# Reordering at a megakernel's joints: an add, a table-loading exponential, routing numbers and the first expert's transposes

## The chip, the cores and the metric

The kernel is one program on 1 core of a Trainium2 chip. Its metric is device time in microseconds (us). A profiled execution gives, beside it, the span of the core's recorded work and the share of full clock that TensorE was granted.

Engines are named as in the profile: PE is TensorE, PEld its weight loads, DVE is VectorE, ACT is ScalarE, POOL is GpSimd, and SP is the engine whose queue issues most loads and stores. Each works through its own queue of instructions in order and waits on semaphores for the others.

## The reference, cut to what matters

Two layers act on x (8, 256, 512), that is T = 2048 rows of 512 numbers, with a context of the same shape.

```python
# layer 0
x = x + (relu(n @ wg) * group_norm(A @ V)) @ wo       # n = layernorm(x); 4 heads of 128, decay-masked A
n = layernorm(x)
h = silu(bitlinear(n, w1)) * bitlinear(n, w3)         # 512 -> 1408
x = x + bitlinear(h, w2)                              # rows rounded to 8 bits, weights to -1, 0, 1
# layer 1
x = x + mlstm(layernorm(x), ctx, ctx)                 # 16 heads of 32, decays are exponentials of gate sums
r = rmsnorm(x) * norm_w
scores = softmax(r @ gate_w); topk_w, topk_ids = top_k(scores, 4)
# 32 experts of width 256; an expert keeps at most 2*N/E of its rows
out = x + routed(r, topk_ids, topk_w) + (silu(r @ sg) * (r @ su)) @ sd
```

## The kernel before, in words

Rows go in 16 tiles of 128 (`NT`), or in 4 chunks of 512 (`NCH`); `D` is 512, `KD` its 4 blocks of 128, `E` 32 experts, `TOPK` 4. `g.X[i]` holds the residual rows of tile `i` in on-chip memory from end to end. The stages follow one another on PE, and each hands over to the next at a joint.

**Layer 0 attention** (`layer0_attention`). For each tile: gate product `pw`, attended heads `po`, normed heads `y`, their product `wy`, its transposes, the output product `pz` (`output`, L431), and `settled` (L437), which adds `pz` to the residual (L438) and takes the row statistics (`norm_stats`, L127). All of it stands inside `tc.manual_schedule`: there the order of the code is the order of the queues of PE, ACT, DVE, POOL and SP. The stage's end is L497 to L510: output of tile 15, statistics of tile 14, tile 1 normed and rounded for the feed-forward (`ffn_normed`, `ffn_rounded` L545, `quantize` L513), the context rows' mean (`centered`), reciprocal roots of the statistics, and `settled(15)` last of all.

`quantize` is five instructions in a chain: the largest magnitude (DVE), two 128x1 operations for the scale `qs` (DVE), a shift by a large constant (ACT), and the subtraction that leaves the rounded row `xq` (DVE). `ffn_turned` then issues a transposing DMA for `xqT`.

**Feed-forward, joined to layer 1** (`layers_joined`). Each tile has three chunks of products `p` (L1203) for two weights in two banks each; the banks (tag `pqk`) alternate between two, so that a third chunk needs the first one's banks back, which come free when `gated` (L1216) has multiplied the Silu of one by the other. The hidden row is rounded (`largest` L1220, `hidden_rounded`) and, two tiles later, multiplied by the second weight (`py`, L1250). During the last tiles the first steps of layer 1 are woven in. After the loop come `hidden_scale(15)` and `shifted` for the last hidden row, and then the rounds of layer 1.

**Layer 1 attention** (`layer1_rounds`). There are 32 blocks. A block makes decays (`pd` on PE, then the exponential `xe` on ACT, L821), weights `ct` (`pqk` on PE, L844 on DVE), heads and a normed rest. A round has places 0 to 4; two dictionaries in `layers_joined`, `places` and `spread`, say what is done besides at a place (round, place): the last tiles' outputs and adds, and turns: `early` and `behind` (L1463) each transpose a normed query tile (`ft`, L1330), copy it, and start a further normed row (`xn`, L1322).

**Choices** (`choices`, from L1501). It finds each row's four experts, their weights, the counts `pc`, the experts' order by count (`order`, then `rank` by a 32x32 comparison and its sum), the places `pp` and from these the numbers of list and slot. It is a generator, and at each `yield` `all` runs `filler()`: a piece of the shared expert of chunks 0 and 1 (products L1060, gated rows `act` L1069, down product `po` L1080). A piece has matmuls and a rest, and the rest waits in `then` until the next piece's matmuls stand.

**Route** (`route`, from L1590). It makes index rows on POOL (`iota`), casts them on DVE, and builds the lists of rows by expert and slot: 8 `to_list` and 64 `to_slot` one-hot matrices (DVE), whose products `pl` (L1654) give `tok_of`, the rows that each expert gathers, and `to`, where its results go. `is_rank`, `at` and `expert` give the experts' numbers, which SP reads to load their weights. Here no order is written out: a planner places the instructions of `route` and of the shared expert's chunks 2 and 3 (`glu` L1744 to L1749, `down` L1761, `add`, store).

**Experts** (`layer1_ffn`, from L1715). `fetch` (L1786) gathers an expert's rows by an indirect DMA from POOL; `turn` (L1792) takes their weights for this expert (`of`, L1796, with a sum), transposes them (`pt`, L1801) and multiplies by the norm's weights (`xT`, L1802). From `tc.manual_schedule` at L1831 on, PE, ACT and DVE follow the code: the first expert's four turns, then 32 experts, each with two products, Silu, `act`, a down product, scaling `eo` and an indirect add into the output (L1805). Ahead of `route`, POOL clears the output's spare rows with a memset and four DMAs.

Of the kernel before, what the change touches and what calls it, by code (L numbers as in the profile page):

```python
# [30 lines left out]
P = 128  # L31
# [212 lines left out]
def layer0_attention(g, tc, cp, qpool):  # L244
# [7 lines left out]
    with ExitStack() as ctx:  # L252
# [178 lines left out]
        def output(i, of=range(KD)):  # L431
            if 0 in of:
                pz[i] = ps.tile([P, D], F32, tag=f"s{2 + i % 2}", name="pz")
            for k in of:
                nc.tensor.matmul(pz[i], lhsT=wyT[i][:, k, :], rhs=wo[:, k, :], start=k == 0, stop=k == KD - 1)  # L435

        def settled(i):  # L437
            nc.vector.tensor_add(g.X[i], pz.pop(i), g.X[i])  # L438
            norm_stats(g, g.mv[:, i, :], g.X[i])

        def raw_load(i):
# [17 lines left out]
        with tc.manual_schedule(engines={E_.PE, E_.Activation, E_.DVE, E_.Pool, E_.SP}):  # L459
            ternary.load_next()  # L460
            ternary.load_next()
            pw[0] = gate(0)
            for h in range(H0 + 1):
                if h < H0:
                    nc.vector.tensor_mul(AT[h], sums[h], AT[h])
                    nc.scalar.activation(AT[h], AT[h], AF.Abs)
                if h:
                    nc.vector.tensor_scalar(AT[h - 1], AT[h - 1], 1.0, None, ALU.max)
            for i in range(NT - 1):
                paired = i in (0, NT - 2)  # L470
                if i != 1:
                    attended(i)
                    ternary.scale_next(i)
                    normed_heads(i)
                ternary.side(i)
                if i:
                    centered(i - 1)
                raw_load(i)
                pw[i + 1] = gate(i + 1)
                if paired:  # L480
                    attended(i + 1)
                if 1 <= i < NT - 3:
                    values((i + 3) // 2, (i + 1) % 2)
                if i:
                    output(i - 1)
                gated(i)
                if paired:
                    normed_heads(i + 1)
                turned(i)
                if i:  # L490
                    settled(i - 1)
                if i == NT - 2:
                    xn = ffn_normed(g, work, 0)
                ternary.clip()
            late = NT - 1
            gated(late)
            output(late - 1, range(KD - 1))  # L497
            turned(late)
            output(late - 1, range(KD - 1, KD))
            g.begun.append(ffn_turned(g, *ffn_rounded(g, work, xn)))  # L500
            ternary.side(late)
            centered(late - 1)
            raw_load(late)
            output(late)
            settled(late - 1)
            ternary.clip()
            g.begun.append(ffn_turned(g, *ffn_rounded(g, work, ffn_normed(g, work, 1))))
            centered(late)
            roots_of_inputs(g, slice(4, NT - 1))
            settled(NT - 1)  # L510


def quantize(g, out, tmp, x):  # L513


    nc = g.nc
    am = g.small.tile([P, 1], F32, tag="am", name="am")
    nc.vector.tensor_reduce(am, x, AX.X, ALU.max, apply_absolute_value=True)
    inv = g.small.tile([P, 1], F32, tag="qi", name="qi")
    nc.vector.tensor_scalar(inv, am, 1e-5, 1.0 / 127.0, ALU.max, ALU.mult)  # L520
    sc = g.small.tile([P, 1], F32, tag="qs", name="qs")
    nc.vector.reciprocal(sc, inv)
    nc.scalar.activation(tmp, x, AF.Identity, bias=g.eps["magic"], scale=sc)
    nc.vector.tensor_scalar(out, tmp, MAGIC, 127.0, ALU.subtract, ALU.min)
    return inv

# [15 lines left out]
    return xn  # L542


def ffn_rounded(g, work, xn):  # L545

    nc = g.nc
    xq = work.tile([P, D], BF16, tag="xq", name="xq")
    ix = quantize(g, xq, xn, xn)
    s13 = g.fin.tile([P, 2], F32, tag="s13", name="s13", bufs=4)  # L550
    nc.vector.tensor_scalar(s13, g.iw[:, :2], ix, None, ALU.mult)
    return xq, s13
# [200 lines left out]
def layer1_rounds(g, tc, gates, work, ps, qp):  # L753
# [390 lines left out]
    class Rounds:  # L1144
# [20 lines left out]
        def all(self, between):  # L1165
            full = len(blocks) + 3
            for n in range(full + 10):
                if n - full in (-2, -1, 0, 1, 2, 4, 6, 7):
                    filler()
                round_(n, between)  # L1170
            lgT = logits()
            filler()
            logits_turned(lgT)
            for _ in choices(g, work, ps):
                filler()
            while pieces or then:
                filler()

# [3 lines left out]
def layers_joined(g, tc, qp, gates):  # L1182
# [5 lines left out]
    with tc.tile_pool(name="f0a1", bufs=2, reuse_waits="tile") as work, tc.tile_pool(name="f0a1ps", bufs=1, space=PSUM, reuse_waits="tile") as ps:  # L1188
# [20 lines left out]
        def silu(t, n):  # L1209
            p1, _, sg = p[n]  # L1210
            return nc.scalar.activation(sg, p1, AF.Silu, scale=xq[t][1])  # L1211
# [135 lines left out]
        with tc.manual_schedule(engines={E_.PE, E_.Activation, E_.DVE, E_.Pool, E_.SP}):  # L1347
# [15 lines left out]
            for t in range(NT):  # L1363
# [52 lines left out]
                gate_steps(t, 2)  # L1416
                products(t, 2)
                behind = silu(t, 2)
                for ins in {8: gates.picked, 11: partial(later_constants, g)}.get(t, tuple)():
                    tc.add_manual_dep(  # L1420
                        ins.ins, behind.ins.name,
                        mybir.DependencyInfo(mybir.DependencyClass.Sync, mybir.DependencyReason.DATA),
                        reason="in this tile's time",
                    )
# [33 lines left out]
            def turned(tag, engine=None):  # L1458
# [7 lines left out]
                (0, 2): [partial(times, 1, first)],  # L1466
                (0, 1): [partial(rooted, late - 2, 5), partial(hidden_rounded, late), partial(rooted, late - 2), partial(added, late - 1)],
                (0, 4): [partial(times, 1, first), norm_next, norm_next],
                (1, 1): [early],
                (1, 3): [behind],  # L1470
                (1, 4): [partial(stats, late - 1), partial(times, 1, first)],
                (2, 0): [partial(output, late, "back", 1)],
                (2, 1): [partial(added, late), early],
# [27 lines left out]
def choices(g, work, ps):  # L1501
# [50 lines left out]
    for i in range(NT):  # L1552
        nc.tensor.matmul(pc, lhsT=onesb, rhs=mask[:, i, :], start=i == 0, stop=i == NT - 1)
    nc.vector.tensor_copy(count, pc)
    nc.vector.scalar_tensor_tensor(order, col, -1.0 / P, count, ALU.mult, ALU.add)
    nc.vector.tensor_tensor(
        sq, order.unsqueeze(1).to_broadcast(square), order.unsqueeze(2).to_broadcast(square), ALU.is_gt
    )
# [28 lines left out]
    yield  # L1587


def route(g, keep, pool, ps):  # L1590


    nc = g.nc
# [10 lines left out]

    lists_i = new("lists_i", [P, E, NJ], I32)
    nc.gpsimd.iota(lists_i, pattern=[[16, E], [1, NJ]], base=0, channel_multiplier=0)
    slots_of = new("slots_of", [P, E])
    for r in range(E):
        if r == 0 or SLOTS[r] != SLOTS[r - 1]:
            nc.gpsimd.memset(slots_of[:, r:], float(SLOTS[r]))  # L1610
    col = new("col", [P, E])
    nc.vector.tensor_copy(col, iota[:, :E])

    slots = new("slots", [P, P], F16)
    nc.vector.tensor_copy(slots, iota)
    lists = new("lists", [P, E * NJ], F16)
    nc.vector.tensor_copy(lists, lists_i.rearrange("p e j -> p (e j)"))
    row = new("row", [P, 1])
    nc.vector.tensor_copy(row, iop)
    number = new("number", [P, NT])  # L1620
    nc.vector.tensor_scalar(number, col[:, :NT], float(P), 1.0, ALU.mult, ALU.add)
    nc.vector.tensor_scalar(number, number, row, None, ALU.add)
    spare = new("spare", [P, NJ])
    nc.vector.tensor_scalar(spare, col[:, :NJ], float(P), float(T + 1), ALU.mult, ALU.add)
    nc.vector.tensor_scalar(spare, spare, row, None, ALU.add)


    g.is_rank = new("is_rank", square, pool=keep)
    nc.vector.tensor_tensor(
        g.is_rank, rank.unsqueeze(1).to_broadcast(square), col.unsqueeze(2).to_broadcast(square), ALU.is_equal  # L1630
    )
    sq = new("sq", square)
    nc.vector.tensor_mul(sq, g.is_rank, col.unsqueeze(1).to_broadcast(square))
    at = new("at", [P, E])
    nc.vector.tensor_reduce(at, sq, AX.X, ALU.add)
    g.expert = new("expert", [P, E], I32, keep)
    nc.vector.tensor_copy(g.expert, at)


    pl = ps.tile([P, E, NJ], F32, tag="rt", name="pl", bufs=1)  # L1640
    half = NT // 2
    for n in range(2 * TOPK):
# [6 lines left out]
        for i in range(i0, i0 + half):  # L1649
# [5 lines left out]
                pl.rearrange("p e j -> p (e j)"), lhsT=to_slot, rhs=to_list[:, i - i0, :],  # L1655
                start=n == 0 and i == 0, stop=n == 2 * TOPK - 1 and i == NT - 1,
            )


    plf = new("plf", [P, E, NJ])  # L1660
# [54 lines left out]
def layer1_ffn(g, tc):  # L1715
    nc = g.nc
    with ExitStack() as ctx:
# [47 lines left out]
            return [po[h * at : h * at + n, :cols] for h in range(parts)]  # L1765

        zero = work.tile([P, D], F32, tag="eo", name="zero", bufs=3)
        nc.gpsimd.memset(zero, 0.0)
        for j in range(NJ):
            nc.gpsimd.dma_start(out=g.out[T + j * P : T + (j + 1) * P, :], in_=zero)  # L1770
        sg_w, su_w, sd_w = g.shared
        ps = ctx.enter_context(tc.tile_pool(name="f1ps", bufs=2, space=PSUM, reuse_waits="tile"))
        with tc.tile_pool(name="f1rwork", bufs=1, reuse_waits="tile") as rwork:
            route(g, rp, rwork, ps)
        for c in range(EARLY, NCH):
            act = glu(ps, sg_w, su_w, g.qT[c])
            for j in range(CH // P):
                i = c * (CH // P) + j
                (po,) = down(ps, act, sd_w, j)
                nc.vector.tensor_add(g.X[i], po, g.X[i])  # L1780
                nc.sync.dma_start(out=g.out[i * P : (i + 1) * P, :], in_=g.X[i])

        def fetch(r, j, n=P):

            xg = work.tile([P, D + E], F32, tag="xg", name="xg", bufs=6)
# [31 lines left out]
        def turn_block(r, j):  # L1817
# [8 lines left out]
            if r + 2 < E and j < len(BLOCKS[r + 2]):  # L1826
                xg[r + 2].append(fetch(r + 2, j, BLOCKS[r + 2][j]))

        before = []
        E_ = mybir.EngineType  # L1830
        with tc.manual_schedule(engines={E_.PE, E_.Activation, E_.DVE}):  # L1831
            for j in range(NJ):
                turn_block(0, j)
            for r in range(E):
                w13, w2 = load_expert(r)
                act = glu(ps, w13[:, :, :FI], w13[:, :, FI:], xT.pop(r), SLOTS[r], partial(turn_block, r + 1))
# [140 lines left out]
```

## Time and profile before

| | before |
|---|---|
| median of 3 runs | 1031.09 us (1029.36 to 1031.83) |
| profiled execution | 1030.34 us |
| its span | 1028.6 us, 14755 instructions |
| mean granted PE clock | 0.994 |
| busy PE, PEld | 990.8 us (96%), 603.4 us |
| busy DVE, ACT, POOL | 527.2, 404.1, 404.5 us |
| HBM read, written | 110.42 MB, 33.23 MB |

By stage, from the same execution (busy us in each stretch):

| stretch, us | what runs | PE | DVE | ACT |
|---|---|---|---|---|
| 200 to 300 | end of layer 0 attention, feed-forward | 94.85 | 89.41 | 68.00 |
| 300 to 400 | feed-forward's end, layer 1 attention's start | 91.04 | 72.80 | 66.87 |
| 400 to 500 | layer 1 attention | 97.18 | 84.07 | 73.08 |
| 500 to 600 | shared expert, choices, lists | 95.55 | 80.39 | 18.46 |
| 600 to 800 | experts | 200.00 | 38.65 | 40.05 |
| 800 to 1000 | experts | 200.00 | 39.59 | 47.37 |
| 1000 to 1028.6 | last expert, end | 17.15 | 2.73 | 3.78 |

How to read it: times are microseconds from the span's start. A row of the timeline or of the chain gives start, duration, engine, line and tile; "x8" is the number of instructions in it, and square brackets hold the idle time before it and what ended that. Matmuls are pipelined, so a busy PE is not PE at its peak, and two rows of matmuls may overlap by a little.

### The profile page before, as it was taken

The numbers are of one execution on the slowest core, as the hardware profiler recorded it, in microseconds if no ns is written. First come the engines' busy times: TensorE is split into PE (matmuls) and PEld (weight loads), VectorE is DVE, ScalarE is ACT, GpSimd is POOL, SyncE is SP. The second block draws the span as 40 slices with busy tenths as digits, with TensorE's granted clock in tenths as the row PEclk, the third lists the DMA queues.
The fourth block names the chain that finished last, engine by engine and source line by source line (L and its number), as shares of the span: only waits on it lengthen the run. The fifth ranks groups of instructions, "written<-read, shape, count | busy, mean of one in ns | idle before, by whom it ended". The sixth has DMA issues, their size and how long they took to land.

```text
span 1028.6 us, 14755 instructions
## 1 busy us (share of the span) xinstructions
PE 990.8 (96%) x5220; PEld 603.4 (59%) x5220; DVE 527.2 (51%) x1338; ACT 404.1 (39%) x693; POOL 404.5 (39%) x501
## 2 busy tenths in 40 slices
PE   8999999989999899999999999999999999999995
PEld 6766656534444356666544445555666666778783
DVE  7446566679987858878969831211212221122110
ACT  4443343457776757877430002122122222221221
POOL 0023443430111113788303225455455555444432
PEclk9999999999999999999999999999999999999998
DMA  9853333324332511231116248687788788889983
GB/s 344 294 185 117 141 118 130 103 67 76 60 58 40 92 39 45 64 126 55 62 62 225 82 147 189 169 209 190 182 207 207 207 210 231 220 242 240 230 225 46
DMA packets 101154, 152.67 MB, mean 148 GB/s; under 512 B 39592, under 2 KB 42280, under 8 KB 101036
## 3 DMA queue, kind: packets, MB, share of 16 engines
q1 hardware_dynamic: 82128, 107.04, 34.1%
q0 software_dynamic: 18944, 44.60, 19.4%
q8 instruction: 43, 0.70, 0.3%
q14 instruction: 39, 0.32, 0.1%
HBM read 110.42 MB, written 33.23 MB: 140 GB/s over the span
## 4 chain that ended last, share of the span: by engine, by line
PE 72%; DVE 13%; DMA 4%; POOL 4%; ACT 3%; issue 2%; SPq 0%; POOLq 0%; ACTq 0%; DVEq 0%
PE po L1761 14%; PE pg L1744 13%; PE pu L1744 13%; PE pw L399 5%; PE pz L435 5%; PE pt L1801 3%; PE p L1203 2%; DMA wst<-in_w1T 2%; DVE am L1220 2%; PE pgu L1060 2%; DVE h L1216 2%; DVE ct L844 2%; PE po L415 1%; PE po L412 1%; DVE st L127 1%
## 5 line engine op out<-in xcount | busy, mean ns | idle before, releaser
L1749 DVE TENSOR_TENSOR act<-pu,sg 128x264 f32<-128x264 f32 (+22 forms) x68 | 31.9, 469 | 313.5 <-PE pu L1744 303.2
L1786 POOL DMA_INDIRECT xg<-h_d,tok_of x85 | 83.6, 983 | 196.0 <-DVE of L1796 64.1
L1805 POOL DMA_INDIRECT out_x<-eo,to x85 | 132.9, 1564 | 55.1 <-ACT eo L1843 34.3
L1761 PE MATMUL po<-w,act 128*128 128x512 f32 (+10 forms) x456 | 143.1, 489 | 0.0
L1744 PE MATMUL pg<-xT,w 128*128 128x216 f32 (+21 forms) x512 | 134.9, 406 | 0.7 <-DVE xT L1802 0.7
L1843 ACT ACTIVATE eo<-po,slotw 128x512 f32<-128x512 f32 (+10 forms) x114 | 65.1, 576 | 173.9 <-PE po L1761 166.9
L1744 PE MATMUL pu<-xT,w 128*128 128x216 f32 (+21 forms) x512 | 133.3, 403 | 0.0
L1744 PEld LDWEIGHTS pg<-xT,w 128*128 128x128 f32 x512 | 93.2, 190 | 33.2 <-issue 16.9
L1748 ACT ACTIVATE sg<-pg 128x264 f32<-128x264 f32 (+22 forms) x68 | 28.5, 420 | 213.5 <-PE pg L1744 213.5
L1744 PEld LDWEIGHTS pu<-xT,w 128*128 128x128 f32 x512 | 96.8, 190 | 26.2 <-issue 5.6
L1203 PE MATMUL p<-wq,xqT 128*128 128x512 bf16 (+1 forms) x384 | 82.9, 367 | 6.4 <-DVE qi L1224 3.1
L1761 PEld LDWEIGHTS po<-w,act 128*128 128x128 f32 (+10 forms) x456 | 54.1, 155 | 57.5 <-issue 47.6
L420 POOL TENSOR_TENSOR y<-y,gam 128x512 f32<-128x512 f32 x16 | 20.2, 1265 | 135.5 <-DVE y L81 135.5
L1203 PEld LDWEIGHTS <-xqT 128*128 128x128 bf16 x384 | 37.6, 99 | 50.2 <-issue 13.6
L1802 DVE TENSOR_TENSOR xT<-pt,nw 128x512 f32<-128x512 f32 (+12 forms) x85 | 51.1, 601 | 20.5 <-PE pt L1801 20.5
L435 PE MATMUL pz<-wo,wyT 128*128 128x512 f32 x128 | 57.8, 594 | 0.7 <-ACT wyT L429 0.7
L399 PE MATMUL pw<-wg,xnT 128*128 128x512 f32 x128 | 57.8, 594 | 0.0
L1801 PEld LDWEIGHTS pt<-ident,xg 128*128 128x128 f32 (+15 forms) x340 | 39.1, 140 | 23.6 <-PE po L1761 10.5
L127 DVE BATCH_NORM_STATS2 st<-x 128x6 f32<-128x512 f32 x64 | 43.8, 687 | 9.2 <-POOL x L913 4.5
L1801 PE MATMUL pt<-ident,xg 128*128 128x128 f32 (+15 forms) x340 | 47.0, 260 | 0.6 <-DVE xT L1802 0.5
L844 DVE SCALAR_TENSOR_TENSOR ct<-pqk,xe 128x768 f32<-128x768 f32 x44 | 40.0, 951 | 8.8 <-PE pqk L840 8.1
L1211 ACT ACTIVATE sg<-p,s 128x512 f32<-128x512 f32 (+1 forms) x48 | 31.1, 648 | 28.2 <-PE p L1203 28.1
(338 smaller groups left out, 1678.7 us busy)
## 6 DMA issues: line engine op xcount, KB each, us to landing
w<-in_w SPq DMA_DIRECT2D x32, 1024.0 KB
w<-in_w SPq DMA_DIRECT2D x32, 512.0 KB
wst<-in_w1T SPq DMA_DIRECT2D x8, 704.0 KB
wst<-in_w3T SPq DMA_DIRECT2D x8, 704.0 KB
wst<-in_w2T SPq DMA_DIRECT2D x6, 768.0 KB
x<-in_x SPq DMA_DIRECT2D x16, 256.0 KB
ctxT<-in_ctxT_d SPq DMA_DIRECT2D x4, 1024.0 KB
raw<-in_ctx SPq DMA_DIRECT2D x16, 256.0 KB
```

The costliest lines, as they stand in the source:

```text
L127: first = g.nc.vector.bn_stats(st, x)
L399: nc.tensor.matmul(pw, lhsT=xnT[c][:, k, o : o + P], rhs=wg[:, k, :], start=k == 0, stop=k == KD - 1)
L435: nc.tensor.matmul(pz[i], lhsT=wyT[i][:, k, :], rhs=wo[:, k, :], start=k == 0, stop=k == KD - 1)
L844: nc.vector.scalar_tensor_tensor(ct[:, r : r + 2, :], pqk[:, :, : S + P], 1.0 / math.sqrt(HD1), xe[:, r : r + 2, :], ALU.mult, ALU.mult,)
L1203: nc.tensor.matmul(both[:, m, : z - a], lhsT=xqT[:, k, :], rhs=w[:, k, a:z], start=k == 0, stop=k == KD - 1)
L1744: nc.tensor.matmul(pp[:, :n], lhsT=w[:, k, cols], rhs=xT[:, k, :n], start=k == 0, stop=k == KD - 1)
L1761: nc.tensor.matmul(po[h * at : h * at + n, :cols], lhsT=act[:, m, j * P : j * P + n], rhs=w[:, m, h * cols : (h + 1) * cols], start=m == 0 ...
L1786: nc.gpsimd.indirect_dma_start(out=xg[:n], out_offset=None, in_=h_d, in_offset=bass.IndirectOffsetOnAxis(ap=g.tok_of[:n, r, j : j + 1], ax ...
L1801: nc.tensor.transpose(pt[:, k, :n], xg[:n, k * P : (k + 1) * P], g.ident[:n, :n])
L1802: nc.vector.tensor_mul(xT, pt[:, :, :n], g.nw.unsqueeze(2).to_broadcast([P, KD, n]))
L1805: return nc.gpsimd.indirect_dma_start(out=g.out, out_offset=bass.IndirectOffsetOnAxis(ap=rows, axis=0), in_=eo, in_offset=None, compute_op ...
L1843: nc.scalar.activation(eo[:n, at : at + cols], po, AF.Copy, scale=w[r][:n, j : j + 1])
```

## The change

It has six parts. No instruction's shape changes, and nothing is left out of the computation.

1. `settled` is split. The add of `pz` becomes `summed`, and that of tile 15 is handed through `ffn_rounded` to `quantize`, which runs it between tile 1's shift on ACT and its rounding on DVE. The statistics of tile 15 stay at the end.
2. After the last tile's last Silu, ACT takes an exponential of a constant (128x1).
3. The first turn, `early` at place 1 of round 1, goes to place 3, ahead of `behind`.
4. `choices` yields once more, right after `order`; at that yield only the waiting rest of a piece is run, and no new matmuls.
5. `route` clears the spare rows behind the index rows on POOL, casts `lists` and `slots` first, and makes `spare`, `is_rank`, `at` and `expert` inside the first pass of the list loop.
6. The gathers of the first two experts and the first expert's four turns stand ahead of the down product of tile 14, instead of behind all shared rows.

The diff, cut to its core:

```diff
+        def summed(i):
+            nc.vector.tensor_add(g.X[i], pz.pop(i), g.X[i])
         def settled(i):
-            nc.vector.tensor_add(g.X[i], pz.pop(i), g.X[i])
+            if i in pz:
+                summed(i)
             norm_stats(g, g.mv[:, i, :], g.X[i])
...
-            g.begun.append(ffn_turned(g, *ffn_rounded(g, work, ffn_normed(g, work, 1))))
+            g.begun.append(ffn_turned(g, *ffn_rounded(g, work, ffn_normed(g, work, 1), partial(summed, late))))
...
     nc.scalar.activation(tmp, x, AF.Identity, bias=g.eps["magic"], scale=sc)
+    if between:
+        between()
     nc.vector.tensor_scalar(out, tmp, MAGIC, 127.0, ALU.subtract, ALU.min)
...
-            for _ in choices(g, work, ps):
-                filler()
+            for only_rest in choices(g, work, ps):
+                if not only_rest:
+                    filler()
+                elif then[0]:
+                    then[0]()
+                    then[0] = None
...
                 behind = silu(t, 2)
+                if t == NT - 1:
+                    nc.scalar.activation(g.small.tile([P, 1], F32, tag="sd", name="warm"), g.eps["ln"], AF.Exp)
...
-                (1, 1): [early],
-                (1, 3): [behind],
+                (1, 3): [early, behind],
...
     nc.vector.scalar_tensor_tensor(order, col, -1.0 / P, count, ALU.mult, ALU.add)
+    yield True
...
     nc.gpsimd.iota(lists_i, pattern=[[16, E], [1, NJ]], base=0, channel_multiplier=0)
+    zeros()
...
-    g.is_rank = new("is_rank", square, pool=keep)
...
-    nc.vector.tensor_copy(g.expert, at)
...
+        if n == 0:
...
+            g.is_rank = new("is_rank", square, pool=keep)
...
+            nc.vector.tensor_copy(g.expert, at)
...
+                if i == NT - 2:
+                    for first in range(NJ):
+                        turn_block(0, first)
                 (po,) = down(ps, act, sd_w, j)
...
         with tc.manual_schedule(engines={E_.PE, E_.Activation, E_.DVE}):
-            for j in range(NJ):
-                turn_block(0, j)
             for r in range(E):
```

## The prediction

> **What bounds the kernel now.** I read the page first (busy shares, chain), then the busy time and granted clock of each stage, then the timeline of the four places that the diff touches.
>
> ```profile
> PE 72%; DVE 13%; DMA 4%; POOL 4%; ACT 3%; issue 2%; SPq 0%; POOLq 0%; ACTq 0%; DVEq 0%
> ```
>
> The chain that ends last is mostly TensorE (PE). The stretches from 600 to 1000 us are 100% busy on PE: the experts only shift with whatever comes before them. So I look for idle PE at the joints. First joint, feed-forward's start (timeline of PE, then windows: length, PE busy, granted clock, DMA share, GB/s):
>
> ```profile
> 215.44 1.90 PE L1203 MATMUL p<-wq,xqT 128*128 128x512 bf16 x8
> 219.86 0.38 PE L1203 MATMUL p<-wq,xqT 128*128 128x512 bf16 x1 [2.52 <-DVE x L438]
> ```
> ```profile
> 216.80:220.22 3.42, 0.90 (x5) 1.00 0.70 148
> 220.22:223.63 3.41, 3.41 (x11) 0.50 0.50 107
> 356.75:360.16 3.41, 1.74 (x16) 1.00 1.10 115
> 360.16:363.58 3.42, 3.42 (x22) 0.50 0.01 3
> ```
>
> PE stood 2.52 us until the add of the last output product freed its bank, and after that window, with 0.90 of 3.42 us busy, the clock was 0.50 for 3.41 us: the next eight matmuls ran 0.43 us apart, not 0.215. The same pair of windows comes at 357 to 363 us. Second joint, the attention's start (the first line from ACT's timeline, the others from the chain of waits):
>
> ```profile
> 350.42 1.28 ACT L821 ACT_TABLE_LOAD   x1 [1.30 <-PE pd L817]
> ```
> ```profile
> 357.75 0.80 ACT xn L1322
> 358.55 0.49 ACT xe L821
> 359.08 0.38 PE pd L816
> ...
> 360.80 1.04 PE ft L1330 x4
> ```
>
> The exponential's table is loaded only after the first decays' matmul. The third `pd` waits for an exponential that stands behind two normed rows on ACT. Third joint, choices and lists:
>
> ```profile
> 560.00:580.00 20.00, 20.00 (x83) 9.28 (x83) 20.00 (x59) 1.20 (x2) 0.00 (x0) 1.00 0.21 78
> 541.11 6.28 PE L1080 MATMUL po<-sw,act 128*128 128x512 f32 x14 [1.39 <-DVE act L1069]
> 554.60 0.68 PE L1654 MATMUL pl<-to_list,to_slot 128*128 128x128 f16 x3 [1.21 <-DVE to_slot L1651]
> ```
>
> In the window line the third busy figure is VectorE (DVE): 20.00 of 20.00. It runs from 537.0 to 584.4 us with no gap over 0.1 us. Fourth joint, the first expert:
>
> ```profile
> 588.75 0.19 DVE L1796 SCALAR_TENSOR_TENSOR of<-xg,is_rank 128x32 f32<-128x32 f32 x1 [3.13 <-DMA xg<-h_d,tok_of]
> 588.86 0.08 DVE L1796 DVE_READ_ACCUMULATOR of<-xg,is_rank 128x1 f32 x1
> 589.09 0.69 DVE L1749 TENSOR_TENSOR act<-pu,sg 128x512 f32<-128x512 f32 x1
> ```
>
> One slot weight (`of`, which waits for its gathered rows) already stands ahead of the last shared `act` on DVE.
>
> **Part 1, the last output product's add.** It moves from 219.13 to behind `qs` of tile 1 (ends 216.27); its product ended at 215.43 (10 matmuls from 210.84, 4.59). It then ends at 216.9, before PE's first eight matmuls do (217.34), so the second chunk starts at 217.4 and ends at 219.1 (8 x 0.215). What is late next: the third chunk takes the first one's banks, so it needs the gated rows `h` of the first. Silu ends at 219.38 (ACT, unchanged), but on DVE `h` stands behind `xq`, the mean, and the statistics of tile 15. The add, 0.6 us, now pushes `xq` from 217.22 to about 217.5, and the rest by about 0.2; after the mean (0.67) and small ones the statistics start at 219.3 where they started at 219.84, and `h` runs 220.15 to 220.9 where it ran 220.67 to 221.39. Third chunk: 220.95, where it was 223.3 (219.86 + 8 x 0.43). That is **-2.35 us**; PE stands 1.8 us instead of 2.52. The second tile's transposing DMA is issued 0.3 later, at 218.1; the first tile's took 2.57 from issue (212.87) to matmul (215.44), so it lands at 220.7 and is wanted at 222.25: hidden by the third chunk (1.3 us), without which it would cost nothing until 0.2. DVE's later rows (`xq` of tile 2 at 224.57, the largest of `h` at 226.10) shift alike, so the loop keeps it. Without the half clock in a run of before, its third chunk would start at 221.6 and the gain be 0.65. Both ends, -0.65 and -2.35, go into the range; I take the traced one.
>
> A page bears here: the Trainium skill, "TensorE: Matmul & The Clock Gate", table "Why this matters for your kernels", says that PE idle of more than about 3 us brings the half clock. The trace has it after 2.52 us, so the row decides. By the page alone the half clock would not come from this gap, and the gain would be an estimated 0.65.
>
> **Part 2, the early exponential.** It pulls the 1.28 us load to 349.13, behind the last Silu. ACT idles there (1.30), and the first decays come 1.0 us sooner, at 350.7. I cost it at nothing: from 349.80 to 357.00 the chain is DVE alone (largest of `h`, add, statistics, reciprocal roots in Newton steps, `nb`), and no step of it waits for ACT; the rounded hidden row at 354.83 follows a root step begun at 354.71 (0.17) while ACT's shift ended at 354.24. The cover is that DVE chain; without it, the part is worth -1.0. Below nothing it can't go by more than the small exponential, 0.3 (like the 128x1 root of 0.30 at 207.56).
>
> **Part 3, the first turn.** Four transposes (`ft`, 1.04 for this set, at half clock; 0.45 at full clock, as the next set has it in the chain at 365.79) leave a hole at 357.89, where PE waited anyway: the third `pd` stays at 359.08, since its exponential still follows both normed rows on ACT. They now stand behind the scores, ahead of the last product `py`. So PE's chain to `py` grows by 0.45 to 1.04; with the clock halved for one window in both, I get +0.3 (the idle before it grows to 3.4 us, 355.7 to 359.08, so a half clock is as good as certain). `copy` of that turn on DVE moves behind two `ct` (1.82), into 2.23 us that DVE stood before the add at 365.83: nothing. Normed rows 10 on ACT wait for the moved transposes (two buffers), and the second copy ends about when `py` starts: 0 to 0.1. **+0.3** (0 to +1.0).
>
> **Part 4, gated rows.** `act` (0.69) goes ahead of the comparison and its sum (1.23, 1.22). PE's 1.39 vanishes; DVE's sum to the lists is the same. PE is not what ends here: 0.
>
> **Part 5, lists' numbers.** DVE runs the same operations before `tok_of` in either order (64 `to_slot`, 8 `to_list`, 3 `act`, 7 adds), so `tok_of` still ends near 583.98: 0. The first `to_slot` comes about 2.3 sooner (552.2), but PE reaches it at 549.0 (14 x 0.43 from 539.6, 8 x 0.43), since only four rows of `pg` now stand ahead: 3.2 us idle in place of 1.39 + 1.21, with 2.6 us more work behind it, in a stretch where PE has some 2 us of slack against DVE. A half clock there (1.7 us of lost work) would be mostly covered: 0 to +0.5. POOL: the four zero DMAs (1 MB, 2.18 us of issue) go 0.95 us later, behind the index rows; POOL is idle 32.1 us after that. SP: the experts' numbers come 3.4 us later (556.6), so 3 MB of weights are issued at 557.4 and land near 569 rather than 565.3; wanted at 599.4. That cover is 30 us.
>
> **Part 6, the first expert's turns before the last two tiles.** Removed: after the last product PE spent 3.3 us (596.13 to 599.44) on 16 transposes (1.8) and waits for `xT` (0.51 + 0.05 + 0.74 + small). Now three rows of product (2.6) cover the four `xT` (0.6, 0.6, 0.6, 0.42). Added wait: on DVE three `of` stand ahead of the last `act`. Fetches are issued at 584.27, 585.69, 586.97; the first two took 4.5 and 4.8 to land (588.75, 590.5), the range of all is 2.8 to 4.8, so the third lands at 590.7 to 591.8 (below: 589.8). I take 591.1. `act` ends at 591.8 instead of 589.78; behind it on DVE stand the adds and `xT`, and PE waits for it after one row. From 588.98: 0.86 + 2.0 wait + 7 x 0.86 + 1.8 = 599.7, against 599.44. **+0.4** (-1.3 if nothing waits; +1.0 with the latest landing; half clock +1.7 more).
>
> **Sum.** -2.35 + 0 + 0.3 + 0 + 0.1 + 0.4 = -1.5 us on an execution of 1030.34 (span 1028.6 and 1.74 around it): 1028.8. The median of the three runs, 1031.09, lies 0.75 higher; I forecast half way, **1029.2**.
>
> **Rivals.**
> - Fetches in time: if the second and third gathers land by 589, `act` does not wait and part 6 is -1.5, part 3 nothing: -2.35 - 1.5 = -3.9, 1026.5 to 1027.2. For it: gathers of 2.8 us exist, and fewer writes run beside them. Against: 4.5 and 4.8 are those of this place.
> - The wait takes the gain back: three `of` hold `act` to 592.5 and the clock halves after it. Place: DVE's queue at 589. It decides from a landing of the third fetch past 591.5, PE then stands over 2.5 us as at 217. Price: 1.0 + 1.7; with the small form of part 1 (-0.65), part 3 at 1.0 and part 5 at 0.5: +3.5, 1034.6. For it: the 3.13 us wait is there now. Against: PE had 0.86 us of its own work.
> - The change does nothing as a whole: part 1 is worth only 0.65, and parts 3 and 6 give it back: 0, about 1031.
>
> **How the numbers follow.** Forecast 0.40, in-time fetches 0.30, wait 0.18, nothing 0.12. A difference below 0.3% (3.1 us) can't be told from none here: faster means under 1028.0, slower over 1034.2. Of the forecast's own spread (part 2 or 3 better by 1.0) I count 0.09 as faster: faster 0.39, same 0.31 + 0.12 = 0.43, slower 0.18. The range leaves out about one in ten at each end: 1026.5 to 1033.5; the forecast's own is 1027.5 to 1031.
>
> **What would show it.** Right: no wait of PE on DVE's `x` add near 217, no half clock near 220, third chunk near 221; an ACT table load right behind the last Silu; the last shared `act` near 591 with a PE gap of 2 us ahead of it; experts' first `pg` 1.5 us sooner. Wrong: PE's chain from 220 to 350 not shifted by 2 us; `tok_of` moved by over 1 us against the choices' first row; `act` at 589.

## The result, and the profile after

The changed kernel takes 1032.59 us (median of 20 runs, 1029.84 to 1035.19); the kernel before, in 20 runs, 1029.64 us (1027.52 to 1032.0). The ratio is 1.0027, 95% interval [1.0018, 1.0035]. The medians lie 2.95 us apart: the kernel became slower, where 1.9 us faster than the three runs then shown (median 1031.09) was forecast. The profiled execution took 1033.24 us, span 1031.5 us, granted clock 0.991. Its span is 2.9 us over the one of before, as the medians are, so the two profiles are a fair pair.

The chain of waits at its end, from the page of the changed kernel, has less PE and more VectorE, DMA and issue:

```profile
PE 70%; DVE 14%; DMA 5%; POOL 4%; ACT 3%; issue 3%; SPq 1%; POOLq 0%; DVEq 0%; ACTq 0%
```

Windows of the changed kernel (length, PE busy, granted clock, DMA share, GB/s), in pairs: a joint, and what follows it.

```profile
216.80:220.22 3.42, 2.63 (x13) 1.00 0.65 151
220.22:223.63 3.41, 1.89 (x10) 1.00 0.78 128
353.88:357.29 3.41, 0.41 (x3) 1.00 0.56 107
357.29:360.71 3.42, 3.15 (x21) 0.50 0.02 6
548.44:551.85 3.41, 0.24 (x2) 1.00 1.02 374
551.85:555.27 3.42, 3.42 (x9) 0.50 0.14 49
589.40:592.81 3.41, 1.32 (x4) 1.00 0.79 230
592.81:596.23 3.42, 3.10 (x4) 0.50 0.30 90
```

The half clock near 220 is gone, as forecast. Two new ones have come, behind the idle PE at the lists (552) and at the last shared `act` (593), and the one of the attention's start is there as before. PE's timeline shows the four places:

```profile
215.80 3.63 PE L1213 MATMUL p<-wq,xqT 128*128 128x512 bf16 x16
221.08 1.46 PE L1213 MATMUL p<-wq,xqT 128*128 128x384 bf16 x8 [1.65 <-DVE qi L1234]
223.21 3.63 PE L1213 MATMUL p<-wq,xqT 128*128 128x512 bf16 x16 [0.67 <-DMA xqT<-xq]
...
357.56 0.59 PE L822 MATMUL pd<-right,left 128*128 128x512 bf16 x1 [3.28 <-ACT xe L827]
...
551.61 0.51 PE L1650 MATMUL pl<-to_list,to_slot 128*128 128x128 f16 x2 [3.26 <-DVE to_slot L1647]
...
593.13 4.36 PE L1773 MATMUL po<-sw,act 128*128 128x512 f32 x6 [2.42 <-DVE act L1761]
602.42 3.28 PE L1756 MATMUL pg<-xT,w 128*128 128x464 f32 x8
```

The second chunk runs without a wait, the third starts 5.28 us after the first where it took 7.47. The first expert's `pg` is at 602.42 where it was 599.44. VectorE's timeline shows the third `of` ahead of the last shared `act`:

```profile
589.03 0.19 DVE L1803 SCALAR_TENSOR_TENSOR of<-xg,is_rank 128x32 f32<-128x32 f32 x1 [3.07 <-DMA xg<-h_d,tok_of]
591.06 0.19 DVE L1803 SCALAR_TENSOR_TENSOR of<-xg,is_rank 128x32 f32<-128x32 f32 x1 [1.83 <-DMA xg<-h_d,tok_of]
592.28 0.19 DVE L1803 SCALAR_TENSOR_TENSOR of<-xg,is_rank 128x32 f32<-128x32 f32 x1 [1.01 <-DMA xg<-h_d,tok_of]
592.39 0.69 DVE L1761 TENSOR_TENSOR act<-pu,sg 128x512 f32<-128x512 f32 x1
```

**A ledger of the joints.** Instructions on VectorE that every profile holds (1338 records in each) mark the joints. Feed-forward's start runs from tile 14's add (213.69 before) to the largest of tile 1's `h` (232.92), attention's start from `nb` (356.83) to the last feed-forward add (365.83), the last one from the counts' copy (537.01) to the first expert's `act` (606.04). Outside these stretches nothing behind the start differs by over 0.2 us. The table gives what each stretch took over that of before, for all runs, and where the clock was halved (ahead of the last 15 us). "Start" is what an execution had lost before tile 14's add; it varies by up to 1.9 us with nothing changed there, and is seen from 55 us on. Every row is one execution.

| run | start | feed-forward's start | attention's start | choices to first expert | half clock near |
|---|---|---|---|---|---|
| before | 0 | 0 | 0 | 0 | 220, 360 |
| after | +0.36 | -1.83 | +0.73 | +3.70 | 357, 552, 593 |
| part 1 (e1) | +0.31 | -1.97 | +0.11 | +0.18 | 357 |
| part 3 (e2) | +1.42 | +0.25 | +0.56 | +0.31 | 221, 361 |
| parts 4, 5 (e3) | +0.87 | -0.11 | -1.43 | +1.72 | 221, 553 |
| part 6 (e4) | +1.36 | -1.38 | 0.00 | +2.09 | 360, 592 |
| after, `of` behind (e5) | +1.40 | -1.72 | -0.68 | +0.03 | 552 |
| parts 4, 5, filled (e6) | +1.80 | +0.14 | -0.05 | +0.34 | 221, 361 |
| before, gap filled (e7) | +0.04 | -1.36 | +0.01 | -0.01 | 359 |
| after, hole filled (e8) | +1.01 | -1.91 | +1.35 | +1.34 | 12 |
| part 4 (e9) | -0.01 | -1.38 | -1.43 | -0.19 | none |
| part 5 (e10) | -0.11 | +0.16 | -0.07 | +3.66 | 219, 359, 554, 602 |
| parts 1, 6 mended (e11) | +0.12 | -2.22 | -1.43 | -1.45 | none |
| mended (e12) | +0.12 | -1.83 | +0.86 | -0.75 | 356 (two windows), 547 |

The row "after" adds up to +2.96, the spans differ by 2.9.

### The profile page after: what moved, and what is told of

The parts are those of the page before. It is cut to its first block, busy times and chain, and to the rows that moved or that the text cites. A ratio compares the mean times of both kernels' runs of the same rounds, so it can differ in the third digit from the quotient of the medians.

```text
span 1031.5 us, 14751 instructions
## 1 busy us (share of the span) xinstructions
PE 990.7 (96%) x5220; PEld 604.2 (59%) x5220; DVE 527.4 (51%) x1338; ACT 404.1 (39%) x694; POOL 404.3 (39%) x501
## 4 chain that ended last, share of the span: by engine, by line
PE 70%; DVE 14%; DMA 5%; POOL 4%; ACT 3%; issue 3%; SPq 1%; POOLq 0%; DVEq 0%; ACTq 0%
PE po L1773 14%; PE pu L1756 13%; PE pg L1756 12%; PE pw L399 5%; PE pz L435 5%; PE pt L1808 3%; PE p L1213 2%; DMA wst<-in_w1T 2%; DVE am L1230 2%; PE pgu L1066 2%; DVE h L1226 2%; DVE ct L850 1%; PE po L415 1%; PE po L412 1%; PE pqk L842 1%
## 5 line engine op out<-in xcount | busy, mean ns | idle before, releaser
L1260 PE MATMUL py<-wq,hq 128*128 128x512 bf16 x176 | 40.6, 379 | 0.8 <-DMA hq<-hq 0.5
```

## The experiments

**Theory A**: each joint pays for itself and PE carries the sum to the end; the losses are parts 4 and 5 (rows taken from ahead of the first list product), part 6 (the wait of `of`) and part 3, each with a half clock behind the idle PE. **Rivals**: the gain of part 1 is lost again downstream; one joint holds the whole loss; or VectorE's `tok_of`, not PE, decides. Ratios are to the kernel before, run in the same session; "joint" is the ledger's figure for the stretch that the edit changes.

**e1, part 1 alone.** Edit: of the diff only `partial(summed, late)` and what it needs.

> The kernel before with part 1 alone (the last output product's add between tile 1's shift and its rounding). Theory A, each joint pays on its own and PE carries it to the end: the profile of the changed kernel has the third chunk at 221.08 where it was 222.91, with 0.37 us lost before both at 55 us, and then 0.67 us of waiting for the second tile's transposed rows; so this part is worth 1.8 to 1.9 us, ratio about 0.9982, and the first expert's product starts near 597.6 instead of 599.44. Rival B, the gain is lost again at a later joint (choices or lists, where VectorE decides) and all of the measured 2.95 us comes from there: first expert's product within 0.3 us of 599.44, ratio 1.000.

Ratio 0.9997 [0.9988, 1.0006]; the profile's first expert is 1.41 us sooner (`pg` at 598.02). The ledger has the 1.97 us, and nothing takes them back later. So the trace has theory A, but the times are nearer the rival's 1.000, and their interval leaves theory A's 0.9982 out; e4 and e7 give part of the reason.

**e2, part 3 alone.** Edit: `(1, 1): [early]` goes, `(1, 3): [early, behind]`.

> The kernel before with part 3 alone (the first turn moved from place 1 to place 3 of round 1). Theory A: PE stands some 3.2 us ahead of the third decays' product, the products behind it run at half clock, and the attention's PE chain is 0.7 us later from 364 us on (the changed kernel was 1.51 us ahead at 357.6 and 0.78 ahead at 365): ratio about 1.0007, which is at the edge of what the times can tell; the trace decides. Rival: the moved transposes only fill a hole later, 0 to 0.3 us, and the 0.7 us belonged to part 2's earlier table load.

Ratio 1.0015 [1.0003, 1.0026]; attention's start +0.56. The size is theory A's, its cause isn't: with the half clock in both orders the step is +0.56 and +0.73; without it in either, the old order has -1.43 (e3, e9, e11) and the new one -0.68 (e5), 0.75 apart again. (The changed kernel and e5 hold part 2 as well, e2 doesn't.) The chain of waits of the changed kernel names it:

```profile
360.19 0.86 PE ft L1340 x4
...
361.14 0.81 ACT xn L1332
361.95 0.48 ACT qT L1351
362.43 0.04 issue
362.47 2.53 PE py L1260 x11
```

The last output product `py` takes the bank that the second turn's copy must leave; that copy stands behind a normed row (0.81) on ACT, which waits for the moved transposes. So `py` comes four transposes and a wait later, at any clock (0.43 and 0.35 in e5, at full clock).

**e3, parts 4 and 5 alone; e9, part 4; e10, part 5.** Edits: the hunks of `choices` and of `route`, each by itself.

> The kernel before with parts 4 and 5 alone (gated rows at the additional yield; lists' numbers in another order). Theory A: PE comes to the first list product about 3 us early, stands, runs the next rows at half clock and has 2.6 us more work behind that point, so the last shared up product ends 1.6 us later and the first expert starts 1.6 us later, near 601.0: ratio about 1.0016. Rival 1, VectorE's queue decides: tok_of is about 0.9 us later (the changed kernel went from 0.51 ahead to 0.43 behind) and so is the first expert: ratio 1.0009. Rival 2, the recorded forecast: 0 to 0.1 us.

> The kernel before with part 4 alone (gated rows at the additional yield). Part 5's order of the numbers is as before, so PE's queue keeps seven rows between the last down product and the first list product. Theory A (the loss of parts 4 and 5 comes from the rows that part 5's order takes from ahead of the first list product): counted from the counts' copy, the first expert comes within 0.4 us of before, since the idle that goes at the gated rows comes back at the first to_slot (2.6 us in one piece, perhaps with a half clock). Rival: the early yield is what costs (the gated rows stand ahead of the comparison on VectorE): 0.7 us or more later.

> The kernel before with part 5 alone. Theory A: PE's queue has four rows instead of seven ahead of the first list product, so the first expert comes 1.2 to 1.7 us later, counted from the counts' copy; parts 4 and 5 together had 1.72. Rival (part 4 costs): 0 to 0.4 us.

e3: 1.0027 [1.0014, 1.0039], joint +1.72. e9: 1.0000 [0.9990, 1.0009], joint -0.19. e10: 1.0018 [1.0005, 1.0031], joint +3.66, of which 1.70 lie behind the last shared `act`, where one more half clock came (601.76 to 605.18); up to that `act` it is +1.96, a little over the 1.2 to 1.7 expected. So part 5 costs and part 4 does not. PE's timeline of part 5 alone:

```profile
547.14 3.60 PE L1754 MATMUL pg<-qT,sw 128*128 128x512 f32 x8
552.57 0.45 PE L1648 MATMUL pl<-to_list,to_slot 128*128 128x128 f16 x2 [1.84 <-DVE to_slot L1645]
552.86 1.08 PE L1754 MATMUL pu<-qT,sw 128*128 128x512 f32 x2
553.77 0.44 PE L1648 MATMUL pl<-to_list,to_slot 128*128 128x128 f16 x4
554.01 3.62 PE L1754 MATMUL pu<-qT,sw 128*128 128x512 f32 x4
```

Eight matmuls of `pg` stand ahead of the first list product, where before had six of `pu` too, and four of `pu` then take 3.62 us at half clock; four of `pg` took 1.94 at full clock.

**e6, the queue filled again.** Edit, on parts 4 and 5: `pg` and `pu` of shared chunk 2's first half are issued ahead of `route`.

```diff
+        begun = [pair_of(ps, sg_w, su_w, g.qT[EARLY], CH, 0)]
         with tc.tile_pool(name="f1rwork", bufs=1, reuse_waits="tile") as rwork:
             route(g, rp, rwork, ps, zeros)
```

> The kernel before with parts 4 and 5, and with the first two products (gate and up, 3.4 us) of shared chunk 2 written ahead of the route, so that PE's queue holds eight rows between the last shared down product and the first list product, where parts 4 and 5 alone have four. Theory A (what parts 4 and 5 cost is PE idle ahead of the first list product, the half clock behind it, and the work pushed behind it): no idle over 1 us near 550, no half clock near 552.5, and the last shared up product comes 1.2 to 1.7 us sooner than with parts 4 and 5 alone, that is from 0.5 us sooner to 0.3 later than before, counted from the logits; ratio about 1.000. Rival: VectorE decides and its tok_of is late by itself in the new order (0.9 us in the changed kernel), then the first expert stays about 0.9 us later than before, counted from the logits.

Ratio 0.9996 [0.9985, 1.0007]; joint +0.34, no half clock at the lists. PE still stands 2.18 us, now ahead of `pg` for its banks, where under 1 was expected. `tok_of` is still 1.00 us later from the counts on, and the first expert only 0.34, as the last shared `pu` is: PE's rows decide, not VectorE's last number. That ends this rival.

**e4, part 6 alone.** Edit: the hunk that moves the shared rows and the turns.

> The kernel before with part 6 alone (gathers' three slot weights and the first expert's turns ahead of the last two shared rows). Theory A: the third gather, issued at 586.97, lands 4.9 us later, the last shared act ends at 592.6, PE stands over 2.5 us and its next six products run at half clock: first expert's product near 602.0, 2.6 us later, ratio about 1.0025. Rival, the recorded forecast of this part: landing near 591.1, no half clock, 0.4 us later, ratio 1.0004. Rival 2: the transposes ahead of the shared rows are what costs, not the wait; then act is on time at 589.1 and the first expert is later all the same.

Ratio 1.0022 [1.0013, 1.0031]; joint +2.09, half clock from 592.16. VectorE's and PE's timelines:

```profile
591.16 0.19 DVE L1802 SCALAR_TENSOR_TENSOR of<-xg,is_rank 128x32 f32<-128x32 f32 x1 [0.48 <-DMA xg<-h_d,tok_of]
591.28 0.68 DVE L1759 TENSOR_TENSOR act<-pu,sg 128x512 f32<-128x512 f32 x1
592.02 4.54 PE L1771 MATMUL po<-sw,act 128*128 128x512 f32 x6 [2.33 <-DVE act L1759]
```

The third gather came earlier than theory A had it, where the recorded forecast of this part put it (591.16 against 591.1), and the half clock came all the same: the wait of 2.33 us lies within one window (588.75 to 592.16, PE busy 1.08), and the clock was 0.50 in the next. Beside that, this profile holds an accident worth more: its feed-forward's start is that of before, the same 2.52 us of wait, and no half clock followed. Timeline and windows of this run:

```profile
221.22 3.19 PE L1213 MATMUL p<-wq,xqT 128*128 128x512 bf16 x16 [2.52 <-DVE x L438]
```
```profile
216.70:220.11 3.41, 1.94 (x8) 1.00 0.72 173
220.11:223.53 3.42, 2.31 (x12) 1.00 0.59 101
```

The half clocks begin and end on a grid of 3.41 us (360.06 and 592.16 lie 68 steps apart). Here the wait falls across a line of that grid, 1.4 us in one window of 3.41 us and 1.1 in the next; in the profile of before it lay within one (0.90 of 3.42 busy). So the same code loses 1.38 us or not, by where the wait lies on the grid. The start (+1.36 here) isn't all of that: e9 started as before did (-0.01), but its grid lay 0.96 us earlier, and the half clock stayed away there too. Without the half clock, part 1 is worth 0.36 to 0.86 us (-1.72 to -2.22 against -1.36 to -1.38).

**e7, the wait filled.** Edit, on the kernel before: 12 matmuls into a spare bank ahead of the second chunk.

> The kernel before, untouched but for 12 extra matmuls (128x512, results not used) between the first tile's first and second chunk, in the 2.52 us in which PE waits for the add near 217. Theory A (the half clock of 220 to 223.6 is what the wait costs, and it comes only in some executions: one other profile of the same stretch, that of part 6 alone, has the same wait and no half clock there): third chunk 1.72 us after the second's start in every execution, first expert 1.3 us sooner than in the profile of before; in the times only the share of executions with a half clock there counts, so 0.3 to 1.3 us, ratio 0.9987 to 0.9997. Rival: the wait itself is the cost; then nothing changes, ratio 1.000, or the extra work delays the second chunk.

Ratio 1.0000 [0.9988, 1.0012]; profile: no half clock, -1.36, third chunk at 221.63, 1.72 after the second. The price of the half clock is shown by this and e4; how often it comes in timed runs isn't. In the seven profiles with this code unchanged it came in five (before, e2, e3, e6, e10; not in e4 and e9), while the times of e1 and e7 leave room for about 1.2 us at most. The mean granted clocks of the timed runs don't settle it either: e1 0.9952 where before had 0.9944 in the same session, e7 0.9942 where it had 0.9945. This stays open.

It bears on the sum as well. The ratios of e1 to e4 add up to 0.61% slower, where the whole has 0.27%, further apart than the intervals together allow. In the profiles the joints that these parts change add up to 2.40 us, where the changed kernel has 2.60. So the ledger prices one execution each, and not what a part is worth in the median run.

**e5, the slot weights behind the last `act`.** Edit, on the changed kernel:

```diff
+                if r == 0:
+                    tc.add_manual_dep(weighed.ins, g.acted.ins.name, ...)
```

> The changed kernel, but the first expert's four slot weights are ordered behind the last shared act on VectorE; the transposes stay ahead of the last two shared rows. Theory A (the wait of the slot weights for their gathers is what part 6 costs, through an idle PE and the half clock behind it): act starts right after the last shared up product, near 589.9, no half clock near 593, 16 rows of product and 16 transposes follow in 9 us, and the first expert's product starts near 598.8 to 599.2 where the changed kernel has 602.42: 3.2 to 3.6 us better than the changed kernel, ratio to before about 0.9995. Rival: the gathers land too late for the transposes as well (second gather at 591.0, third at 592.2), so PE waits at the transposes instead and the first expert comes near 601 to 602 all the same, ratio about 1.002.

Ratio 0.9996 [0.9986, 1.0007], where the changed kernel has 1.0027; first expert's `pg` at 598.65, 0.15 ahead of the range. PE's timeline has no gap from 589.6 on:

```profile
589.60 3.86 PE L1773 MATMUL po<-sw,act 128*128 128x512 f32 x8
593.30 1.04 PE L1814 MATMUL pt<-ident,xg 128*128 128x128 f32 x8
594.17 1.02 PE L1773 MATMUL po<-sw,act 128*128 128x512 f32 x2
595.10 1.09 PE L1814 MATMUL pt<-ident,xg 128*128 128x128 f32 x8
596.03 2.78 PE L1773 MATMUL po<-sw,act 128*128 128x512 f32 x6
598.65 3.28 PE L1756 MATMUL pg<-xT,w 128*128 128x464 f32 x8
```

The gathers land as late as in the changed kernel (third `of` at 592.58, there 592.28), and the transposes do not wait for them: the rival falls.

**e8, the hole of part 3 filled.** Edit, on the changed kernel: 14 matmuls at place 1 of round 1.

> The changed kernel with 14 extra matmuls (128x512, results not used) at the place that the first turn left, ahead of the third decays' product, where PE stands 3.28 us. Theory A (part 3 costs by the half clock that follows the idle PE): full clock at 357.6, the scores, two turns and decays behind it take 3.6 us instead of 4.9, and everything from 365 on is 0.7 to 0.9 us sooner than in the changed kernel; ratio to before about 1.0019. Rival: the turn's place itself costs (it stands on PE's path in place 3 as it did not in place 1): no gain.

Ratio 1.0037 [1.0022, 1.0051]. A miss: ACT's copy of `pmT` waited 5.00 us, until the fill had ended, and with it the normed rows and the exponential behind it, so the third decays' product came at 360.13. But this profile has no half clock between 15 us and the end, and so shows part 6's wait without it (PE's timeline):

```profile
593.47 2.84 PE L1779 MATMUL po<-sw,act 128*128 128x512 f32 x6 [2.50 <-DVE act L1767]
```

The wait is 2.50 us, and six products take 2.84 us where the changed kernel's took 4.36. From the counts on it lost 1.34 us instead of 3.70, of which 0.76 stand at the last shared `pu`; so part 6 costs 0.58 us without the half clock and about 2.0 with it. (At the lists PE stood 3.37 us in this profile, ahead of `pg` instead of behind it, across two windows.)

**e11, parts 1 and 6 with the slot weights behind; e12, all but part 3, with both mendings.**

> The kernel before with part 1, and with part 6 whose slot weights are ordered behind the last shared act. If the ledger by joints adds up: part 1 0.45 (no half clock near 220 in the run compared) to 1.9 us, part 6 mended 1.6 us sooner: first expert near 596.0 plus what the start loses at 55 us (0 to 1.8 us in the profiles); time 2.0 to 3.4 us under before, ratio 0.9967 to 0.9981, faster than both kernels. Rival: the gathers land too late without the later tok_of of the changed kernel, or the times show only part of what a profile shows: ratio 0.999 or above.

> The changed kernel without part 3, with the slot weights behind the last shared act, and with shared chunk 2's first two products written ahead of the route. By the ledger: part 1 0.45 to 1.9 us sooner, lists 0.34 us later, part 6 mended 1.6 us sooner; ratio 0.9970 to 0.9985, within 0.05% of the two parts alone. Rival: the filled queue and the mended part 6 do not go together (PE has the same rows left behind the last list product), and the first expert is 1 us or more later than with the two parts alone.

e11: 1025.91 us (median of 6 runs), 0.9968 [0.9956, 0.9980], faster than both kernels; PE's first expert `pg` is at 594.49 and no half clock stands ahead of the end. Of its profile's 5.1 us (2.22 + 1.43 + 1.45), the 1.43 is a half clock near 360 that this execution missed, as e3 and e9 did, and no gain of the edit. e12: 0.9982 [0.9973, 0.9991], above e11 by 0.14% where 0.05% was expected, though the intervals overlap. The filled queue makes PE wait 2.18 us for banks at 547, and the half clock comes there instead. That is the smaller part of what its profile has over e11's: 2.29 of the 3.1 us stand at the attention's start, where the clock was halved for two windows (355.82 to 362.65). With part 2 and the old order of turns, PE's decays stand earlier there and it waits 2.10 us ahead of the transposes, in e11 1.66. Part 2 was never run alone, so whether it makes the half clock likelier isn't shown.

## Why the prediction was wrong, step by step

- **Part 1** (-2.35): in the profile -1.83. The third chunk came as worked out (5.28 us after the first; 220.95 was forecast, 221.08 less the 0.36 of the start is 220.72). But before had it at 222.91 and not at 223.3: of the eight matmuls from 219.86 on, the first ran at full clock and the second in part, so only 2.19 were gained there. Mis-sized, too, was what is late next: the second tile's transposed rows, "lands at 220.7 ... hidden", were issued at 218.19 and let PE start at 223.21, 5.0 us later where the first tile's took 2.57; PE waited 0.67. The term also took one execution's half clock for the code's: without it the step is worth 0.36 to 0.86 (-0.65 was the other end).
- **The page cited there** (the Trainium skill, "TensorE: Matmul & The Clock Gate", table "Why this matters for your kernels": idle of more than about 3 us brings the half clock) was weighed against a single row. The runs say that 2.52 us halve the clock if they lie in one window and do not if they lie in two, and that 2.33 us in one window are enough (e4), so about 3 us is too long as a bound here; the row alone decided too much.
- **Part 2** (0): right as far as the runs show. The load ended at 348.90, 1.3 us sooner against VectorE's chain, and `nb` stands where it stood in that chain: VectorE's chain covers it. Not foreseen was that earlier decays leave PE idle for longer ahead of the third one: 3.28 us in the changed kernel, 2.85 in e2.
- **Part 3** (+0.3, bounds 0 to +1.0): +0.73. The mechanism was named (transposes ahead of `py`, normed rows on ACT waiting for them); mis-sized was "the second copy ends about when `py` starts: 0 to 0.1", which is 0.35, and the netting against the half clock, which both orders share. The idle of 3.4 us was misread: PE's rows of before end at 356.35 and not at 355.7, so part 3 leaves 2.7, and e2 has 2.85; the rest is part 2's.
- **Part 4** (0): right, -0.19 alone.
- **Part 5** (about +0.1): failed, +1.72 with part 4. The 3.2 us of idle and the 2.6 us of rows pushed behind were both seen (3.26 measured). The step that failed is "in a stretch where PE has some 2 us of slack against DVE ... would be mostly covered". VectorE's full 20.00 of 20.00 was read as slack on PE's side, though the same line has PE at 20.00 too, and PE's rows behind the last list product are on the path: their end came 1.68 us later, and 0.76 later where no half clock came (e8). That `tok_of` would not move was wrong as well: from the counts on it came 1.24 later, 1.00 with the queue filled (e6), and with it the gathers; it was one of the signs of being wrong that were named.
- **Part 6** (+0.4): +2.09 alone. The wait, its place and even the price of "half clock +1.7 more" stood in the text (1.5 measured). What failed is the step that kept the half clock out of the sum: it was to decide only "from a landing of the third fetch past 591.5", with PE standing over 2.5 us. In e4 the fetch landed as taken (`of` at 591.16), PE stood 2.33 us, and the half clock came. In the changed kernel the landing failed too: issued 0.4 us later, at 587.37, for the later `tok_of`, and 4.9 us under way, it let `of` start at 592.28, and PE stood 2.42 us.
- **The sum and the chances.** The rival "the wait takes the gain back" had 0.18 and 1034.6; its mechanism is what came. Its +3.5 lies near the ledger's +2.96 partly by luck: part 1 was 1.2 us better than it took, and part 5 1.2 worse. Three idle stretches of 2.4 to 3.3 us were left or made on PE, and a half clock was priced at only one of them as likely.

## What to carry to other kernels

When a queue is reordered, list every stretch in which the bounding engine will stand idle for two microseconds or more, and price the slower clock behind each, not only the wait. A full engine does not give the other one slack: count what is left on each after their last handover. An instruction that waits for a transfer goes behind whatever the next engine needs from the same queue; here one ordering edge turned 2.1 us of loss (e4) into 1.45 us of gain (e11).

## What the runs showed of the hardware

- Half clocks start and end on a grid of 3.41 us, and follow a window in which PE was busy for little. Over the fourteen profiles, without the first 16 and the last 15 us, all sixteen windows with 1.32 us or less of PE were followed by half clock; from 1.46 to 1.87 us either came (1.74 was followed by it at 356.75 of the kernel before, 1.72 at 349.91 was not); above that, two were: 2.11 us in e10 (598.35 to 601.76) and 3.04 in e12, in a window that was itself at half clock. So the bound is not sharp by this measure. One half clock costs 1.4 to 1.5 us in work that fills it (1.38 at 220, 1.43 at 360, 1.5 at 593).
- Most of what differs from run to run goes with it: over the 20 runs of the changed kernel, time and mean granted clock have a correlation of -0.89, from 1029.84 us at 0.995 to 1034.85 at 0.988. The mean clock is 0.9921 there and 0.9944 in 33 runs of before; 0.0023 of 1030 us at half speed is 4.7 us, or an estimated 1.4 windows more.
- The first three gathers of the changed kernel took 4.3, 5.0 and 4.9 us from issue to first use, issued 1.3 to 1.4 us apart; those of e4 4.0, 4.9 and 4.3.
